# Turning layer 1's upper blocks by VectorE and DMAs instead of TensorE, with a new order of tokens

## The chip, the cores and the metric

The kernel runs on one core of a Trainium2 chip. The metric is the device time of one execution in microseconds (us); the median of three runs of the kernel before is 3070.16 us (3066.79 to 3072.19). TensorE multiplies matrices, VectorE and ScalarE work on elements and reductions, GpSimd does small arithmetic, and SyncE issues nearly all DMAs, in its program's order.

## The reference

The input x has 4 images of 128 channels and 64 x 64 = 4096 positions, in float32. Layer 0 is a convolutional attention with a gate; layer 1 is a self-attention over the positions as tokens, followed by a normalised recurrence over the tokens.

```
x = x + conv_attention(group_norm(x))              # q, k: 64 channels; v, gate: 128
t = tokens(x)                                      # [4, 4096, 128]
h = layer_norm(t); q = h @ W; scores = q @ q.T     # the scores are symmetric
t = t + softmax(scores) @ h
wx = batch_norm(layer_norm(t) @ Wf.T)
y[i] = sigmoid(wx[i] + y[i-1] @ V.T)               # over the 4096 tokens
x = from_tokens(t + y)
```

## The kernel before, in words

Each image goes through layer0 and layer1, four times in all; then one recurrence runs over all images. Work is tiled in blocks of 512 tokens (QB; NB = 8 per image), each of 4 tiles of 128 tokens (NQ).

Layer 0 (attention, lines 200 to 244, and layer0, 388 to 473) runs over 8 query blocks and 16 pairs of key tiles. Scores (L223) and weighted values (L403) use half the rows of TensorE each, two at a time. When a block ends, its finish appends small functions to the list `pending`: sums, denominators, projection, tokens. One of them is taken after a step of the main loop, which spreads the work; `ahead` holds the preparation of the next image, which takes the steps that `nothing` leaves.

A block is exchanged between channels-by-tokens and tokens-by-channels by `move` (L255 to L266): VectorE turns each 32 x 32 piece (L261), one DMA writes the result to a DRAM tile turn_d (L264), and four DMAs read it back, one for each group of 32 partitions (L266). Layer 0 uses it three times a block: for x, for the projected output, and for the normalised tokens into qt.

Layer 1 (layer1, L475 to L716) uses the symmetry of the scores. For query block n it computes score blocks (n, a) for a from n down to 0 (L672), takes the exponential on ScalarE with a row sum (L678), and multiplies with h (L539, `direct`). For a < n the same block is also needed turned, as (a, n): VectorE turns its pieces into dd (L683), sixteen DMAs on SyncE's queue exchange the 32-row groups into tt (L710), and four steps later TensorE multiplies it with h (L552, `reversed_products`) while VectorE sums it (L557). dd has two buffers and tt three. The order of n is 6, 7, 5, 4, 3, 2, 1, 0. `part` adds a product to oacc (L566) and `count` calls finish(n) when all parts of block n are there. In the last image the pair (1, 0) isn't turned but computed twice (`order`, `turns`).

finish(n) of layer 1 (L579 to L651) appends tokens, result, turn and inputs to `pending`. tokens turns oacc on TensorE (L608, four turns of 128 x 128 into PSUM), divides by the row sums and adds the old tokens (L610), and normalises into h2 (L276 to L280, GpSimd L131 and L132 for the root). result turns the new tokens back on TensorE (L621), copies them on ScalarE (L624) and stores them in t2_d (L625). turn does the same with h2 (L630, L631) into th, and inputs multiplies by the recurrence's weights (L635), takes the statistics (L636) and stores the product (L639 or L643).

A scheduler of the tile framework puts the instructions into each engine's order and sets the waits; an engine then runs its list strictly in order. `fast` and its tiles are set up in conv_attn_hybrid_kernel; the tail after all images is L763 to L850.

Of the kernel before, what the change touches and what calls it, by code (L numbers as in the profile page):

```python
# [10 lines left out]
F32 = mybir.dt.float32  # L11
I32 = mybir.dt.int32
AF = mybir.ActivationFunctionType
ALU = mybir.AluOpType
# [35 lines left out]
def conv_attn_hybrid_kernel(  # L50
# [14 lines left out]
    wxs_d = dram.tile([B, P, L // 2, G, 2], F32, name="wxs_d")  # L65
    t_d = dram.tile([B, NB, P, 4, NQ, 32], F32, name="t_d")

    turn_d = [dram.tile([P, 4, NQ, 32], F32, name=f"turn{i}_d") for i in range(8)]
    t2_d = dram.tile([B, C, N], F32, name="t2_d")
    wx_d = dram.tile([B, C, N], F32, name="wx_d")  # L70

# [86 lines left out]
def fast(  # L158
# [13 lines left out]
    with ExitStack() as st:  # L172
# [79 lines left out]
                nc.tensor.matmul(m[:, r, :cols], lhsT=lhsT[rs], rhs=rhs[rs], start=True, stop=True)  # L252
            return m[:, 0, :cols], m[:, 1, :cols]

        def move(blocks, dst):  # L255

            nonlocal n_moves
            d = work.tile([P, 4, NQ, 32], F32, tag="d", name="d", bufs=2)  # L260
            nc.vector.transpose(d.rearrange("q a j i -> q j a i"), blocks)  # L261
            via = turn_d[n_moves % len(turn_d)]
            n_moves += 1
            nc.sync.dma_start(via, d)  # L264
            for a in range(4):
                nc.sync.dma_start(dst[bass.ts(a, 32)], via[:, a].rearrange("(p i) j k -> i p j k", p=4))  # L266

        n_moves = 0

# [15 lines left out]
        def tiles(t):  # L285

            return [t[:, :, j, :] for j in range(NQ)]

        def quarters(t):
            return [t[:, j, :].rearrange("q (p i) -> q p i", p=4) for j in range(NQ)]  # L290
# [97 lines left out]
        def layer0(b, gate, q, k, v, need):  # L388
# [20 lines left out]
            def finish(n, o, acc):  # L409
                cs, ts = bass.ts(n, QB), bass.ts(n, NQ)  # L410
                og = work.tile([P, QB], F32, tag="og", name="og")
                nc.scalar.copy(og, o[1])
                nc.vector.tensor_tensor(og, o[0], og, ALU.add)
                nc.vector.tensor_tensor(og, og, gate[:, cs], ALU.mult)
                rinv = stat.tile([P, NQ], F32, tag="rinv", name="rinv")
                xb = work.tile([P, QB], F32, tag="xb", name="xb")
                t = work.tile([P, 4, NQ, 32], F32, tag="t", name="t", bufs=2)
                yt = work.tile([P, 4, NQ, 32], F32, tag="h2", name="yt")
                nc.sync.dma_start(xb, x[b, :, cs])
                nc.gpsimd.tensor_scalar(xb, xb, bpc, None, ALU.add)  # L420

                sub = stat.tile([P, NQ, 4], F32, tag="sub", name="sub", bufs=2)

                def sums():


                    half, blocks = acc[:, 0, :], acc[:, 1, :]
                    nc.vector.tensor_tensor(half, half, blocks, ALU.add)
                    nc.vector.transpose(blocks, half)
                    nc.vector.tensor_reduce(  # L430
                        sub, blocks.rearrange("q (j f k) -> q j f k", j=NQ, f=4), AX.X, ALU.add
                    )
                    move(xb.rearrange("c (j f k) -> c j f k", j=NQ, f=4), t)

                def denominators():
                    m0, m1 = halves(quart, sub.rearrange("q j f -> q (j f)"))
                    tot = stat.tile([P, NQ, 4], F32, tag="tot", name="tot", bufs=2)
                    flat = tot.rearrange("q j f -> q (j f)")
                    nc.vector.tensor_copy(flat, m0)
                    nc.vector.tensor_tensor(flat, flat, m1, ALU.add)  # L440
                    nc.vector.tensor_tensor(
                        tot, tot,
                        own.rearrange("q (j f) -> q j f", j=1).to_broadcast([P, NQ, 4]), ALU.mult,
                    )
                    den = den_all[:, b * NT + n * NQ : b * NT + (n + 1) * NQ]
                    nc.vector.tensor_reduce(den, tot, AX.X, ALU.add)
                    nc.vector.reciprocal(rinv, den)

                def projection():
                    m0, m1 = halves(wt["ps"], og)  # L450
                    nc.scalar.copy(og, m1)
                    nc.vector.tensor_tensor(og, m0, og, ALU.add)
                    move(og.rearrange("c (j f k) -> c j f k", j=NQ, f=4), yt)

                def tokens():
                    for j in range(NQ):
                        nc.vector.scalar_tensor_tensor(  # L457
                            t[:, :, j, :], yt[:, :, j, :], rinv[:, j : j + 1], t[:, :, j, :],
                            ALU.mult, ALU.add,
                        )  # L460
                    nc.sync.dma_start(t_d[b, n], t)
                    layernorm(tiles(t), quarters(h[:, ts, :]))

                    move(
                        h[:, ts, :].rearrange("q j (p i) -> q j p i", p=4),
                        qt[:, cs].rearrange("c (p j k) -> c p j k", j=NQ, p=4),
                    )
                    done.add((b, n))

                pending.extend([sums, nothing, denominators, projection, nothing, tokens])  # L470
# [4 lines left out]
        def layer1(b, h, qt):  # L475
# [52 lines left out]
            def order(n):  # L528


                return [0, 1] if b == B - 1 and n == 0 else list(range(n, -1, -1))

            def turns(n, a):
                return a < n and not (b == B - 1 and n == 1)
# [37 lines left out]
            def count(n):  # L572


                parts[n] += 1
                if parts[n] == NB - (b == B - 1 and n < 2):
                    finish(n)

            def finish(n):  # L579
                cs = bass.ts(n, QB)  # L580
                rinv = stat.tile([P, NQ], F32, tag="rinv", name="rinv")
                t = work.tile([P, 4, NQ, 32], F32, tag="t", name="t1", bufs=2)
                if b == B - 1 and n == 0:

                    one, two = (ep.tile([P, 2, QB], F32, tag="e", name="last") for _ in range(2))
                    h2, t1 = (one[:, r, :].rearrange("q (j c) -> q j c", j=NQ) for r in range(2))
                    th, t2 = two[:, 0, :], two[:, 1, :]

                    def bank():
                        return ps_s.tile([P, 2, QB], F32, tag="s", name="ml")[:, 0, :]  # L590
                else:
                    h2 = work.tile([P, NQ, C], F32, tag="h2", name="h2")
                    th = work.tile([P, QB], F32, tag="th", name="th")
                    t1 = work.tile([P, NQ, C], F32, tag="og", name="t1b")
                    t2 = None

                    def bank():
                        return ps_m.tile([P, QB], F32, tag="m", name="m1")
                nc.sync.dma_start(t, t_d[b, n])

                def tokens():
                    at = (B + b) * NT + n * NQ
                    den = den_all[:, at : at + NQ]
                    nc.vector.tensor_reduce(den, slots[:, bass.ts(n, NQ), :], AX.X, ALU.add)
                    nc.vector.reciprocal(rinv, den)
                    m = bank().rearrange("q (j c) -> q j c", j=NQ)
                    for j in range(NQ):
                        nc.tensor.transpose(m[:, j, :], oacc[:, n, bass.ts(j, P)], ident)  # L608
# [6 lines left out]
                    layernorm(quarters(t1), quarters(h2))  # L615

                def result():
                    nonlocal t2
                    m = bank()
                    for j in range(NQ):  # L620
                        nc.tensor.transpose(m[:, bass.ts(j, P)], t1[:, j, :], ident)  # L621
                    if t2 is None:
                        t2 = work.tile([P, QB], F32, tag="xb", name="t2")
                    nc.scalar.copy(t2, m)  # L624
                    nc.sync.dma_start(t2_d[b, :, cs], t2)  # L625

                def turn():
                    m = bank()
                    for j in range(NQ):
                        nc.tensor.transpose(m[:, bass.ts(j, P)], h2[:, j, :], ident)  # L630
                    nc.scalar.copy(th, m)  # L631

                def inputs():
                    m = bank()
                    nc.tensor.matmul(m, lhsT=wt["f"], rhs=th, start=True, stop=True)  # L635
                    nc.vector.bn_stats(bn_st[:, b * NB + n, :], m)  # L636
                    m = m.rearrange("p (g i s) -> p i g s", i=L // 2, s=2)
                    if b == B - 1:
                        nc.vector.tensor_copy(wxs[:, :, b, bass.ts(n, GB), :], m)  # L639
                    else:  # L640
                        wx = work.tile([P, L // 2, GB, 2], F32, tag="wx", name="wx")
                        nc.vector.tensor_copy(wx, m)
                        nc.sync.dma_start(wxs_d[b, :, :, bass.ts(n, GB), :], wx)  # L643

                if b == B - 1 and n == 0:
                    pending.appendleft(tokens)
                    pending.extend([result, turn, inputs])
                elif b == B - 1 and n < 4:
                    pending.extend([tokens, result, turn, inputs])
                else:  # L650
                    pending.extend([tokens, result, nothing, nothing, turn, inputs])  # L651


            for n in [NB - 2, NB - 1] + list(range(NB - 3, -1, -1)):
# [4 lines left out]
                for a in order(n):  # L659
# [4 lines left out]
                    for i in range(2):  # L664
# [31 lines left out]
                        clock += 1  # L696
                        if len(fifo) > LAG:
                            direct()
                            if a == n and i == 0:
                                direct()  # L700
                        if turned and turned[0][0] <= clock:
                            reversed_products()
                        if pending:
# [67 lines left out]
    with ExitStack() as st:  # L771
# [29 lines left out]
        def bank(k, s):  # L801
            return banks[s][k % 3][:, : HB * G].rearrange("p (b g) -> p b g", g=G)
# [450 lines left out]
```

## Time and profile before

| | |
|---|---|
| median of three runs | 3070.16 us |
| the profiled execution, and its span | 3067.95 us, 3066.1 us |
| TensorE busy, matmul instructions | 3000.1 us, 10834 |
| VectorE busy | 1882.3 us |
| ScalarE busy | 1154.7 us |
| L608, L621, L630: turns in PSUM bank m | 124 each, 19.9, 18.9 and 21.1 us, and 4 each in the last block |
| L624 and L631: copies on ScalarE | 32 each, 0.586 us each |
| L261: turn of 128 x 512 on VectorE | 96, 0.70 to 0.71 us each |
| DMAs tt<-dd (L710) | 1776 of 64 KB, 2.0 us to landing |
| DMAs turn_d<-d (L264), t, yt, qt<-turn_d (L266) | 96 of 256 KB, 384 of 64 KB, 2.0 to 2.1 us |
| DMAs t_d<-t and t_d<-last (L625) | 32 of 256 KB |

In the profile's lists a line gives the source line, the engine, the operation, what is written and read, and the count; PE is TensorE, PEld its loading of weights, DVE VectorE, ACT ScalarE, POOL GpSimd, SPq SyncE's queue. A name is given without its number, so that t2_d appears as t_d. A float32 matmul of the program is two instructions in the profile; a turn (L608, L621, L630) is one. The first number after the bar is busy time, then the mean of one in ns, then the engine's idle time ahead of it and what ended it.

### The profile page before, as it was taken

The numbers are of one execution on the slowest core, as the hardware profiler recorded it, in microseconds if no ns is written. First come the engines' busy times: TensorE is split into PE (matmuls) and PEld (weight loads), VectorE is DVE, ScalarE is ACT, GpSimd is POOL, SyncE is SP. The second block draws the span as 40 slices with busy tenths as digits, with TensorE's granted clock in tenths as the row PEclk, the third lists the DMA queues.
The fourth block names the chain that finished last, engine by engine and source line by source line (L and its number), as shares of the span: only waits on it lengthen the run. The fifth ranks groups of instructions, "written<-read, shape, count | busy, mean of one in ns | idle before, by whom it ended". The sixth has DMA issues, their size and how long they took to land.

```text
span 3066.1 us, 32642 instructions
## 1 busy us (share of the span) xinstructions
PE 3000.1 (98%) x10834; PEld 1377.5 (45%) x10834; DVE 1882.3 (61%) x3160; ACT 1154.7 (38%) x2148; POOL 148.3 (5%) x187
## 2 busy tenths in 40 slices
PE   7999999999999999999999999999999999999996
PEld 3444444444444444444444444444444444444443
DVE  6666665655666666655567666655566666455556
ACT  3444433333344443333344443333334444323334
POOL 0000000000000000000000000000000000000000
PEclk9999999999999999999999999999999999999998
DMA  1011143433211123333311113333321112543333
GB/s 52 28 56 56 42 115 86 99 93 92 53 56 55 41 82 96 93 96 92 85 46 61 39 50 112 88 96 93 94 61 52 46 49 90 139 104 93 99 111 159
DMA packets 233171, 241.17 MB, mean 79 GB/s; under 512 B 88480, under 2 KB 144288, under 8 KB 231968
## 3 DMA queue, kind: packets, MB, share of 16 engines
q1 hardware_dynamic: 231984, 238.18, 27.8%
q8 instruction: 89, 1.46, 0.2%
q14 instruction: 90, 0.74, 0.1%
q10 hardware_dynamic: 1008, 0.79, 0.1%
HBM read 65.80 MB, written 56.62 MB: 40 GB/s over the span
## 4 chain that ended last, share of the span: by engine, by line
PE 95%; DVE 3%; ACT 1%; POOL 0%; DMA 0%; issue 0%; ACTq 0%; SPq 0%; DVEq 0%; POOLq 0%
PE o L403 29%; PE o L539 16%; PE ps L223 15%; PE ps L672 14%; PE ot L552 12%; PE m L252 1%; PE m L635 1%; PE mq L497 1%; PE ps L505 1%; PE mp L335 1%; PE mp L370 1%; PE mp L355 1%; DVE ps_r L810 1%; DVE t2s L837 1%; PE m L630 1%; PE m L608 0%
## 5 line engine op out<-in xcount | busy, mean ns | idle before, releaser
L403 PE MATMUL o<-e,nxt 64*128 64x512 f32 x4096 | 964.8, 590 | 0.0
L225 ACT ACTIVATE e<-ps 128x1024 f32<-128x1024 f32 x512 | 521.6, 1025 | 678.2 <-PE ps L223 653.2
L232 DVE TENSOR_TENSOR acc<-acc,e 128x1024 f32<-128x1024 f32 x448 | 547.6, 1222 | 237.4 <-ACT e L225 221.6
L403 PEld LDWEIGHTS o<-e,nxt 64*128 64x128 f32 x4096 | 399.6, 187 | 483.4 <-issue 475.1
L678 ACT ACTIVATE e<-ps,shift 128x512 f32<-128x512 f32 x516 | 350.4, 683 | 670.0 <-PE ps L672 506.1
L539 PE MATMUL o<-e,h 128*128 128x512 f32 x1160 | 539.5, 592 | 0.0
L223 PE MATMUL ps<-nxt 64*128 64x512 f32 x2048 | 535.8, 597 | 2.2 <-ACT e L225 2.2
L672 PE MATMUL ps<-qt 128*128 128x512 f32 x1032 | 490.9, 595 | 2.9 <-ACT qt L498 2.7
L552 PE MATMUL ot<-tt,h 128*128 128x512 f32 x888 | 399.5, 592 | 0.0
L683 DVE STREAM_TRANSPOSE dd<-e 128x512 f32<-128x512 f32 x444 | 287.2, 687 | 87.9 <-ACT e L678 75.3
L539 PEld LDWEIGHTS o<-e,h 128*128 128x128 f32 x1160 | 218.3, 190 | 266.5 <-issue 261.9
L223 PEld LDWEIGHTS ps<-nxt 64*128 64x128 f32 x2048 | 194.4, 187 | 231.2 <-issue 158.9
L672 PEld LDWEIGHTS ps<-qt 128*128 128x128 f32 x1032 | 187.8, 190 | 213.0 <-issue 188.0
L552 PEld LDWEIGHTS ot<-tt,h 128*128 128x128 f32 x888 | 168.0, 190 | 209.5 <-issue 206.8
L557 DVE TENSOR_REDUCE slots<-tt 128x4 f32<-128x2048 f32 x111 | 250.8, 2260 | 9.8 <-DMA tt<-dd 9.2
L566 DVE TENSOR_TENSOR oacc<-oacc,ot 128x512 f32<-128x512 f32 x87 | 59.7, 686 | 187.0 <-PE ot L552 186.9
L131 POOL TENSOR_SCALAR rstd<-mv 128x4 f32<-128x4 f32 x64 | 14.5, 227 | 2429.7 <-DVE mv L277 2429.7
L678 ACT ACTIVATION_READ_ACCUMULATOR e<-ps,shift 128x1 f32 x516 | 101.3, 196 | 0.0
L457 DVE SCALAR_TENSOR_TENSOR t<-yt,rinv,t 128x128 f32<-128x128 f32 x128 | 36.6, 347 | 71.1 <-DMA yt<-turn_d 71.1
L420 POOL TENSOR_SCALAR xb<-xb,bpc 128x512 f32<-128x512 f32 x32 | 60.9, 1904 | 321.0 <-DMA xb<-in_x_dram 311.3
L132 POOL TENSOR_TENSOR rstd<-rstd,mhalf 128x4 f32<-128x4 f32 x64 | 66.4, 1037 | 5.3
L280 DVE TENSOR_SCALAR h<-t,mv,rstd 128x128 f32<-128x128 f32 x128 | 35.7, 344 | 47.0 <-POOL rstd L132 47.0
(160 smaller groups left out, 1659.5 us busy)
## 6 DMA issues: line engine op xcount, KB each, us to landing
tt<-dd SPq DMA_DIRECT2D x1776, 64.0 KB, 2.0
turn_d<-d SPq DMA_DIRECT2D x96, 256.0 KB, 2.0
t_d<-t SPq DMA_DIRECT2D x63, 256.0 KB, 2.0
nxt<-in_x_dram SPq DMA_DIRECT2D x16, 512.0 KB, 5.6
xb<-in_x_dram SPq DMA_DIRECT2D x32, 256.0 KB, 2.9
t<-turn_d SPq DMA_DIRECT2D x128, 64.0 KB, 2.0
yt<-turn_d SPq DMA_DIRECT2D x128, 64.0 KB, 2.0
qt<-turn_d SPq DMA_DIRECT2D x128, 64.0 KB, 2.1
```

Of the source, the lines that this page charges most:

```text
L132: nc.gpsimd.tensor_tensor(dst, dst, mhalf[:, :n], ALU.pow)
L223: nc.tensor.matmul(ps[:, h, :], lhsT=lhsT, rhs=rhs, start=True, stop=True)
L225: nc.scalar.activation(e, ps, AF.Exp, scale=scale)
L232: nc.vector.tensor_tensor(acc, acc, e, ALU.add)
L403: nc.tensor.matmul(o[r], lhsT=v[rs, p + h * PAIRS, :], rhs=e[rs, h, :], start=(p == 0 and h == 0), stop=(p == PAIRS - 1 and h == 1),)
L420: nc.gpsimd.tensor_scalar(xb, xb, bpc, None, ALU.add)
L539: nc.tensor.matmul(o, lhsT=h[:, NQ * a + 2 * i + half, :], rhs=e[:, half, :], start=(a == order(n)[0] and i == 0 and half == 0), stop=(a = ...
L552: nc.tensor.matmul(ot, lhsT=h[:, NQ * n + j, :], rhs=t[:, :, j, :, :].rearrange("q p k j -> q k p j"), start=(j == 0), stop=(j == NQ - 1),)
L557: nc.vector.tensor_reduce(slots[:, bass.ts(n, NQ), a], t.rearrange("q p b k j -> q b p (k j)"), AX.XY, ALU.add,)
L672: nc.tensor.matmul(ps[:, half, :], lhsT=qt[:, bass.ts(at, P)], rhs=qt[:, bass.ts(n, QB)], start=True, stop=True,)
L678: nc.scalar.activation(e[:, half, :], ps[:, half, :], AF.Exp, bias=shift, accum_out=slots[:, at, n : n + 1],)
L683: nc.vector.transpose(d.rearrange("q f b k j -> q k b f j")[:, 2 * i + half], e[:, half, :].rearrange("q (b f j) -> q b f j", b=NQ, f=NQ),)
```

## The change

`move` is written anew on a helper, turn_out. VectorE's turn stays; now four DMAs write, one for each group f of 32 partitions of d, into every row of the DRAM tile at a column offset, and one DMA reads the tile back as it lies. To fit, the order of tokens inside a block is changed in layer 0's views (f before j), in the sums of the denominators and where th is read. turn_out also writes straight to t2_d.

In layer 1, blocks n of 3 and above (4 and above in the last image) now finish through finish_moved: oacc is exchanged by a move (sums), the new tokens are made in place, h2 is exchanged by a move into th, and t goes to t2_d by a turn_out. Two empty places stand between sums and tokens and between tokens and inputs. The other blocks keep the turns of oacc and h2 on TensorE; their new tokens go to t2_d by a turn_out in place of the turn on TensorE, the copy and the store. reciprocals and recurrence_inputs are parts of the old code, now shared.

In the last image, block 0 takes a = 1 before a = 0, and a score block computed twice is counted for block a once its exponentials have been issued, so that finish(1) comes after it.

```diff
-            nc.sync.dma_start(via, d)
-            for a in range(4):
-                nc.sync.dma_start(dst[bass.ts(a, 32)], via[:, a].rearrange("(p i) j k -> i p j k", p=4))
+        def turn_out(blocks, dst):
+            d = work.tile([P, 4, NQ, 32], F32, tag="d", name="d", bufs=2)
+            nc.vector.transpose(d.rearrange("q a j i -> q j a i"), blocks)
+            for f in range(4):
+                nc.sync.dma_start(
+                    dst.rearrange("(a i) m -> i a m", a=4)[:, :, bass.ts(f, P)],
+                    d[bass.ts(f, 32)].rearrange("i a j k -> i a (j k)"),
+                )
+        def move(blocks, dst):
...
+            turn_out(blocks, via)
+            nc.sync.dma_start(dst, via)
...
-                    move(xb.rearrange("c (j f k) -> c j f k", j=NQ, f=4), t)
+                    move(xb.rearrange("c (f j k) -> c j f k", j=NQ, f=4), flat(t))
...
-                return [0, 1] if b == B - 1 and n == 0 else list(range(n, -1, -1))
+                return [1, 0] if b == B - 1 and n == 0 else list(range(n, -1, -1))
...
-                if parts[n] == NB - (b == B - 1 and n < 2):
+                if parts[n] == NB - (b == B - 1 and n == 0):
                     finish(n)
+            def finish_moved(n):
...
+                nc.sync.dma_start(t, t_d[b, n])
+                def sums():
+                    ot = work.tile([P, 4, NQ, 32], F32, tag="og", name="otk")
+                    move(oacc[:, n, :].rearrange("c (j f k) -> c j f k", j=NQ, f=4), flat(ot))
+                def tokens():
+                    reciprocals(n, rinv)
+                    for j in range(NQ):
+                        nc.vector.scalar_tensor_tensor(
+                            t[:, :, j, :], ot[:, :, j, :], rinv[:, j : j + 1], t[:, :, j, :],
+                            ALU.mult, ALU.add,
+                        )
+                    h2 = work.tile([P, 4, NQ, 32], F32, tag="h2", name="h2m")
+                    layernorm(tiles(t), tiles(h2))
+                    th = work.tile([P, QB], F32, tag="th", name="thm")
+                    move(h2.rearrange("q p j i -> q j p i"), th)
+                    turn_out(t.rearrange("q p j i -> q j p i"), t2_d[b, :, cs])
+                def inputs():
+                    recurrence_inputs(n, th, ps_m.tile([P, QB], F32, tag="m", name="mw"))
+                pending.extend([sums, nothing, nothing, tokens, nothing, nothing, inputs])
...
             def finish(n):
+                if n >= (4 if b == B - 1 else 3):
+                    return finish_moved(n)
...
                 def result():
-                    m = bank()
-                    for j in range(NQ):
-                        nc.tensor.transpose(m[:, bass.ts(j, P)], t1[:, j, :], ident)
-                    nc.scalar.copy(t2, m)
-                    nc.sync.dma_start(t2_d[b, :, cs], t2)
+                    turn_out(t1.rearrange("q j (p i) -> q j p i", p=4), t2_d[b, :, cs])
...
                     nc.scalar.copy(th, m)
+                    result()
...
-                    pending.extend([result, turn, inputs])
+                    pending.extend([turn, inputs])
                 elif b == B - 1 and n < 4:
-                    pending.extend([tokens, result, turn, inputs])
+                    pending.extend([tokens, turn, inputs])
                 else:
-                    pending.extend([tokens, result, nothing, nothing, turn, inputs])
+                    pending.extend([tokens, nothing, nothing, turn, inputs])
...
-                            if a == n and i == 0:
+                            if a == order(n)[0] and i == 0:
                                 direct()
+                        if a > n and i == 1:
+                            count(a)
```

## The prediction

> **What bounds the kernel now.** I read the page first, then the groups of TensorE by line and shape, then TensorE's instructions in order of time around one finished block, then SyncE's queue in order of time, because the change takes work from TensorE and gives it to VectorE and to that queue. From the page:
>
> ```profile
> PE 3000.1 (98%) x10834; PEld 1377.5 (45%) x10834; DVE 1882.3 (61%) x3160; ACT 1154.7 (38%) x2148; POOL 148.3 (5%) x187
> ...
> PE   7999999999999999999999999999999999999996
> ...
> DVE  6666665655666666655567666655566666455556
> ...
> PE 95%; DVE 3%; ACT 1%; POOL 0%; DMA 0%; issue 0%; ACTq 0%; SPq 0%; DVEq 0%; POOLq 0%
> ```
>
> TensorE is busy in every slice but the first and last, and 95% of the chain that ended last is its own. So a TensorE instruction taken out is worth its slot, if nothing new makes TensorE wait. The groups of TensorE by shape (busy us, mean ns of one, then idle before it):
>
> ```profile
> L672 PE MATMUL ps<-qt 128*128 128x512 f32 x1032 | 490.9, 595 | 2.9 <-ACT qt L498 2.7
> L630 PE MATMUL m<-ident,h 128*128 128x128 f32 x124 | 21.1, 283 | 2.2 <-DVE h L280 1.8
> L608 PE MATMUL m<-ident,oacc 128*128 128x128 f32 x124 | 19.9, 275 | 0.0
> L621 PE MATMUL m<-ident,t1b 128*128 128x128 f32 x124 | 18.9, 275 | 0.0
> ```
>
> The mean of one (275 ns) is no price, since matmuls overlap. The price is the distance between starts, here around one set of four turns:
>
> ```profile
> 512.56 1.02 PE L539 MATMUL o<-e,h 128*128 128x512 f32 x2
> 513.42 0.60 PE L608 MATMUL m<-ident,oacc 128*128 128x128 f32 x4
> 513.85 1.02 PE L539 MATMUL o<-e,h 128*128 128x512 f32 x2
> ```
>
> Four turns hold TensorE from 513.42 to 513.85, 0.43 us; two 512-wide instructions hold it 0.86 us. SyncE's queue in the last image's layer 1 (start, length, count):
>
> ```profile
> 2633.84 81.94 SPq L710 DMA_DIRECT2D tt<-dd  x125
> 2715.88 0.53 SPq L625 DMA_DIRECT2D t_d<-t  x1
> 2716.51 42.05 SPq L710 DMA_DIRECT2D tt<-dd  x64
> 2758.60 0.58 SPq L599 DMA_DIRECT2D t<-t_d  x1
> 2759.29 10.02 SPq L710 DMA_DIRECT2D tt<-dd  x16
> 2774.05 0.33 SPq L625 DMA_DIRECT2D t_d<-t  x1
> ```
>
> Sixteen issues for one pair of blocks take 10.0 us (0.633 us apart), and from 2633 to 2758 the queue hardly rests. This is the second resource, and the change loads it.
>
> **What the skill says.** The Trainium skill, "VectorE: DVE Perf Modes", section "The three transpose paths": VectorE turns independent 32x32 blocks only, while TensorE turns a whole 128x128 into PSUM. The trace agrees in form: L261 turns 128x512 in 0.71 us and DMAs finish the exchange between partition groups. "DMA: Bandwidth & Descriptors", section "Anatomy of one DMA": a DMA has about 2 us of fixed cost, mostly the wait for completion. The trace agrees: turn_d<-d, yt<-turn_d and tt<-dd all land 2.0 us after issue, and a write followed by its read costs about 4. Same page, "Issuing engines are not separate DMA queues": issuing time on the sequencer is "usually small relative to the DMA itself". Here it is not small: 1776 issues at 0.633 us are 1124 us of SyncE.
>
> **The change part by part.**
>
> *TensorE.* Moved blocks are 5 in each of three images and 4 in the last, 19 of 32; they lose the turns of L608 and L630, and all 32 blocks lose L621. That is 4 x (19 + 19 + 32) = 280 turns, 70 sets at 0.43 = **29.9 us off the path**, with no cover: TensorE has no holes there. In layer 0, half-height matmuls run in pairs, and starts in the trace show 0.31 us lost on entering and again on leaving a full-height one. The built order has 116 such changes instead of 122, so **-1.9 us**. Beside their slots, the sets of L630, L608 and L621 among full-height matmuls start or end late by some 7 us[...]; about 4 us of that belongs to removed sets: **-4 us**.
>
> *ScalarE.* 19 copies of L631 and 32 of L624 at 0.59 us go, 30 us. ScalarE is 38% busy; I count nothing, and if it were on the path this would only help.
>
> *VectorE.* Added: three turns per moved block (sums, h2, t) and one per other block, 19 x 3 + 13 = 70 at 0.70 = 49 us; multiply-adds and normalisation stay in number. It is 60% busy in layer 1 (79.85 of the 133 us from 487 to 620, by the table of windows), so 2.1 us per moved block lies beside TensorE's work. Nothing counted; if VectorE had no room it would be at most 49 us. The new multiply-add waits for its DMA (ot), and behind it stand the turns into dd and the additions that free the banks of ot. In the built order it stands 2.6 us of TensorE work after SyncE's read issue, which lands in about 2.6; about level.
>
> *SyncE.* A moved block adds two moves of five issues and one turn_out of four, and loses one store: 13 net. The nearest row is yt<-turn_d, 64 KB in pieces of 512 bytes too, from DRAM to 32 partitions: 0.43 us, 0.475 from start to start; 13 x 0.475 = **6.2 us**. Other blocks add 3, 1.4 us. A write of this shape by 32 partitions is not in the trace: bounds 0.33 (a single store) and 0.633 (as tt<-dd), so 4.3 to 8.2 us per block. Room: from 487.5 to 774.1 (22 pairs) SyncE needs 22 x 10.13 + about 9 = 232 of 287, 55 free; five moved blocks ask 31, and TensorE gets 8 shorter, leaving 16. In the last image, 2633.8 to 2940.2, it needs 413 x 0.633 + 5 = 266 of 306, 40 free; four moved blocks and a turn_out ask 26, TensorE gets 8 shorter, leaving 6. Pairs now land mostly 6 to 14 us before TensorE reads them (issued to 522.1, landed 523.6, read 532.9), but only 0.4 us before at 2675.0 in the last image. Adding my queue sums and TensorE's slots side by side in the built order, the last image's room falls by about 10 us over the three pairs around each h2 move and then recovers. I charge **+4 us** of TensorE waits there and none in the first three; bounds 0 and 20.
>
> The wait of the read on its four writes is covered in the built order by three tt<-dd issues (1.9 us) between; uncovered it would be 2 us of queue each. The wait of TensorE's L624 on th: 3.4 to 3.8 us of TensorE work follow the read issue, which needs 2.6; covered unless SyncE runs late. If it does, everything on TensorE stands behind it.
>
> *Layer 0's moves.* Same five issues, four writes and one read instead of one and four: 0.34 + 2.0 + 1.4 + 2.0 before, 1.4 + 2.0 + 0.35 + 2.0 after: **0**, bounds -2 and +2 per image.
>
> *The end.* Block 0 of the last image takes key block 1 first, and block 1 is finished only when those scores exist. In the built order block 1's turns now follow the last product; before they stood ahead of four of its instructions (2961.1). VectorE then has both blocks' multiply-add, statistics and normalisation (3.7 us) and a turn in one row. From the last product to the last inputs' matmul was 9.7 us (2965.0 to 2974.7); laid out with the same durations, counted from the last product: addition to 0.9, block 1's multiply-add to 2.0, statistics to 3.3, turn to 4.0, GpSimd's root to 5.3, normalisation with block 0's multiply-add between to 7.3, statistics and block 1's bn_stats (waiting for its matmul) to 9.3, root to 10.7, normalisation and turns to 12.2, copy to 12.8: **+3 us**, bounds 0 and +5. The last store, four issues and 2 us, lands before the bias of the recurrence is ready: 0.
>
> **Sum.** -29.9 - 1.9 - 4 + 4 + 3 = -28.8. The profiled execution took 3067.95 (span 3066.1): 3039.2. The median is 2.2 above it: **3041**.
>
> **Rivals.** *SyncE becomes the bound, slower.* If issues cost 0.633 and each of the two reads stalls the queue for 2 us, a moved block costs 8.2 + 4 = 12.2 us. Five ask 61 of 47 (55 less 8): 14 over, three times; the last image asks 49 + 2 of 32: 19 over. 61 us of TensorE waiting against a saving of 33 (35.8 less the end's 3): 3070 - 33 + 61 = **3098**. Waiting begins at about 9 us a moved block and passes the saving at 10.7 (19 x 10.7 - 171 = 33). For it: the 81.94 us run above. Against: yt<-turn_d at 0.43 and the fill between write and read. *Half is given back.* Slack is used up at each move in the last image and VectorE waits on ot or on dd, 15 us more: **3056**. For: the 0.4 us at 2675. *Nothing comes off*: the turns lay in TensorE's waits, or new ones of 29 us take their place: **3070**. Against: 0.43 us of undisturbed slot.
>
> **How the numbers follow.** Forecast 66%, 3031 to 3052 (SyncE bounds, end, waits); half back 14%; nothing 5%; SyncE bound 15%. The range 3031 to 3067 takes the first two. About 0.2%, 6 us, is what a measurement can tell from no change. Faster 0.80, same 0.05, slower 0.15.
>
> **What would show it.** Right: 52 turns each at the token and h2 lines, none for t; TensorE idle in layer 1 as small as now; th and ot waits under a few us; the new writes near 0.43 us. Wrong: TensorE or VectorE waiting on tt, th or ot by tens of us, writes over 0.6 us, or SyncE without a pause through layer 1; an end stretch longer by over 5 us.

## The result, and the profile after

The changed kernel takes 3141.87 us (median of 4, 3134.9 to 3148.68) against 3069.86 us: a ratio of 1.0235 (1.0211 to 1.026), 72 us slower. The forecast was 3041, with 3031 to 3067 as its range; even the rival that ended slower (3098) was too fast. The profiled execution is the fastest of the four and spans 3132.8 us, 66.7 more than before; the sums below are of this one. From its page, the lines that answer to those shown of the kernel before:

```profile
PE 3004.7 (96%) x10554; PEld 1360.2 (43%) x10554; DVE 1919.3 (61%) x3230; ACT 1125.9 (36%) x2097; POOL 150.1 (5%) x187
...
PE   7999999899999999999999999989999999999985
...
PE 88%; SPq 4%; DVE 3%; ACT 2%; DMA 1%; issue 1%; POOL 0%; DVEq 0%; ACTq 0%
```

The 280 turns are gone (10834 instructions have become 10554), and yet TensorE's share of the chain falls from 95% to 88%: SyncE's queue has 4%, ScalarE 2% instead of 1, and DMAs 1% instead of 0. Two slices inside layer 1 read 8 and no longer 9. TensorE's groups by shape say where it waited (the figures after the second bar are its idle time ahead of the group, and for what):

```profile
L710 PE MATMUL ps<-qt 128*128 128x512 f32 x1032 | 487.4, 597 | 7.8 <-ACT e L716 3.3 <-ACT qt L504 2.7
L558 PE MATMUL ot<-tt,h 128*128 128x512 f32 x888 | 405.4, 600 | 7.7 <-DMA tt<-dd 5.5 <-issue 2.2
L344 PE MATMUL mp<-nxt,w 128*128 128x512 f32 x60 | 34.9, 666 | 6.4 <-DVE nxt L369 2.4 <-DVE nxt L356 1.7 <-DVE wx L631 1.6
L364 PE MATMUL mp<-w,nxt 128*128 128x128 f32 x192 | 34.1, 331 | 20.1 <-DVE nxt L356 15.3 <-DVE nxt L369 4.7
L379 PE MATMUL mp<-nxt,w 128*128 128x512 f32 x48 | 26.4, 631 | 15.6 <-ACT nxt L380 15.6
L624 PE MATMUL mw<-thm,w 128*128 128x512 f32 x38 | 19.4, 592 | 0.0
L676 PE MATMUL m<-ident,h 128*128 128x128 f32 x48 | 10.5, 316 | 10.6 <-DVE h L286 10.6
```

L344, L364 and L379 are the next image's preparation (queries and keys, values, gate; L335, L355 and L370 before). The change doesn't touch them. Before, their lines were:

```profile
L335 PE MATMUL mp<-nxt,w 128*128 128x512 f32 x60 | 31.8, 611 | 2.5 <-DVE nxt L347 2.5
L355 PE MATMUL mp<-w,nxt 128*128 128x128 f32 x192 | 25.6, 276 | 0.0
L370 PE MATMUL mp<-nxt,w 128*128 128x512 f32 x48 | 25.5, 612 | 0.0
```

They waited 2.5 us in all before and wait 42.1 now, nearly always for the VectorE or ScalarE instruction that empties their PSUM bank (for bank m the program has a single buffer of 128 x 512 in PSUM, where TensorE writes its results). The moved blocks' own matmul (L624, mw<-thm) waits for nothing.

The idle column is not the whole loss. I took each distance from one TensorE start to the next and subtracted what that instruction takes in a stream (its slot: 0.427 us for 512 columns, 0.107 for 128, half of that with 64 rows). What is left over sums to 118.2 us before and 215.6 after: +97.4, against 29.9 of slots saved, which makes 67.5, the difference of the spans within 1 us. By place:

| lost time of TensorE, us | before | after |
|---|---|---|
| layer 1 of images 0, 1, 2 | 8.5 each | 33.4, 35.2, 33.0 |
| layer 0 of images 1, 2, 3 | 7.5 each | 10.7, 12.0, 12.0 |
| layer 1 of the last image, with the end | 16.8 | 25.2 |
| ahead of the preparation (L344, L364, L379), all images | 19.3 | 73.9 |

So 76 of the 97 us lie in layer 1 of the images that prepare another, and 55 stand ahead of the preparation itself. The last image, which prepares none, loses only 8 more than before. This is the stretch of TensorE in layer 1 of image 0:

```profile
555.78 0.59 PE L710 MATMUL ps<-qt 128*128 128x512 f32 x1
556.21 1.02 PE L624 MATMUL mw<-thm,w 128*128 128x512 f32 x2
557.07 1.02 PE L710 MATMUL ps<-qt 128*128 128x512 f32 x2
558.62 1.12 PE L344 MATMUL mp<-nxt,w 128*128 128x512 f32 x2 [0.52 <-DVE wx L631]
562.30 2.08 PE L364 MATMUL mp<-w,nxt 128*128 128x128 f32 x8 [2.56 <-DVE nxt L356]
565.16 2.08 PE L364 MATMUL mp<-w,nxt 128*128 128x128 f32 x8 [0.78 <-DVE nxt L369]
568.02 2.08 PE L344 MATMUL mp<-nxt,w 128*128 128x512 f32 x2 [0.78 <-DVE nxt L369]
569.88 4.46 PE L558 MATMUL ot<-tt,h 128*128 128x512 f32 x8
```

Four pieces of the preparation run one after another. All use the one bank m, so each waits until the one ahead of it has been read out. In the kernel before, 1.3 to 8.6 us of other matmuls lay between such pieces (the two of L355 follow at 555.25 and 557.44):

```profile
541.51 1.02 PE L335 MATMUL mp<-nxt,w 128*128 128x512 f32 x2
...
545.80 1.02 PE L335 MATMUL mp<-nxt,w 128*128 128x512 f32 x2
```

Just ahead of the bunch stands mw, a user of bank m as well. Its operand was asked for much earlier, as SyncE's queue shows:

```profile
517.53 18.23 SPq L750 DMA_DIRECT2D tt<-dd  x29
535.86 2.01 SPq L262 DMA_DIRECT2D turn_d<-d  x4
537.97 1.39 SPq L262 DMA_DIRECT2D t_d<-d  x3
539.53 0.34 SPq L272 DMA_DIRECT2D thm<-turn_d  x1
539.91 0.44 SPq L262 DMA_DIRECT2D t_d<-d  x1
540.45 10.01 SPq L750 DMA_DIRECT2D tt<-dd  x16
558.59 0.62 SPq L632 DMA_DIRECT2D wxs_d<-wx  x1
```

The read for th, issued at 539.53, landed at 542.4; mw starts 13.8 us after that. In the first three moved blocks of images 0 to 2 this lag is 12.9 to 15.0 us every time, in the last two 0.2 to 1.8, and in the last image 6 to 11. TensorE was not held up by data: in its list mw simply stands that late. And SyncE, at 550.5, has no more to do than to wait 8.1 us for the store wxs_d<-wx, which needs mw. The table of windows shows what the bunch costs (columns: us, TensorE busy, granted clock, DMA share, GB/s), first before and then after, in the same stretch:

```profile
556.00:590.00 34.00, 34.00 (x99) 1.00 0.35 91
```

```profile
556.00:590.00 34.00, 24.83 (x70) 0.85 0.37 86
```

TensorE loses 9.2 us of 34 to idling, and the clock is lower too. The Trainium skill, "TensorE: Matmul & The Clock Gate", Part 1, says that an idle TensorE falls back to half its clock until it has been busy again, and names an idle window of about 3.4 us for it. The trace agrees on the half: the granted clock is 0.50 from 561.4 to 571.6, and in layer 1 of images 0 to 2 some 67 full-height matmuls take twice their slot (11 us in all; 3 and 0.3 us before). It doesn't need so long a pause here: the longest hole of these stretches is 2.6 us, with short pieces of work between the holes.

My theory after this reading: in the order that was built, a moved block's mw has its turn for bank m as late as if its operand still travelled through SyncE's queue (on the chip it had landed); the preparation is behind it in the same bank, piles up, and then runs piece by piece with every emptying of the bank exposed. The rivals: the moves make VectorE or the DMAs slower for everybody; SyncE's queue is the bound (my forecast's own rival); layer 0's new moves or the last image's order cost the time.

### The profile page after: what moved, and what is told of

It reads as the page before. It is cut to its first block, busy times and chain, and to the rows that moved or that the text cites. A ratio compares the mean times of both kernels' runs of the same rounds, so it can differ in the third digit from the quotient of the medians.

```text
span 3132.8 us, 32678 instructions
## 1 busy us (share of the span) xinstructions
PE 3004.7 (96%) x10554; PEld 1360.2 (43%) x10554; DVE 1919.3 (61%) x3230; ACT 1125.9 (36%) x2097; POOL 150.1 (5%) x187
## 4 chain that ended last, share of the span: by engine, by line
PE 88%; SPq 4%; DVE 3%; ACT 2%; DMA 1%; issue 1%; POOL 0%; DVEq 0%; ACTq 0%
PE o L412 28%; PE o L545 14%; PE ps L223 14%; PE ps L710 12%; PE ot L558 11%; SPq L750 3%; PE m L252 1%; PE mp L364 1%; PE mp L344 1%; PE mq L503 1%; PE mp L379 1%; PE ps L511 1%; DMA tt<-dd 1%; DVE t2s L877 1%; DVE ps_r L850 1%
## 5 line engine op out<-in xcount | busy, mean ns | idle before, releaser
L545 PE MATMUL o<-e,h 128*128 128x512 f32 x1160 | 533.2, 592 | 0.0
L710 PE MATMUL ps<-qt 128*128 128x512 f32 x1032 | 487.4, 597 | 7.8 <-ACT e L716 3.3
L558 PE MATMUL ot<-tt,h 128*128 128x512 f32 x888 | 405.4, 600 | 7.7 <-DMA tt<-dd 5.5
L721 DVE STREAM_TRANSPOSE dd<-e 128x512 f32<-128x512 f32 x444 | 280.5, 681 | 31.5 <-ACT e L716 23.1
L710 PEld LDWEIGHTS ps<-qt 128*128 128x128 f32 x1032 | 189.5, 190 | 244.5 <-issue 200.0
L563 DVE TENSOR_REDUCE slots<-tt 128x4 f32<-128x2048 f32 x111 | 251.1, 2262 | 69.2 <-DMA tt<-dd 55.5
L558 PEld LDWEIGHTS ot<-tt,h 128*128 128x128 f32 x888 | 169.5, 193 | 220.3 <-issue 213.5
L523 ACT ACTIVATE e<-ps,shift 128x256 f32<-128x256 f32 x64 | 29.7, 469 | 110.8 <-PE ps L517 110.8
```

Of the source, the lines that this page charges most:

```text
L545: nc.tensor.matmul(o, lhsT=h[:, NQ * a + 2 * i + half, :], rhs=e[:, half, :], start=(a == order(n)[0] and i == 0 and half == 0), stop=(a = ...
L558: nc.tensor.matmul(ot, lhsT=h[:, NQ * n + j, :], rhs=t[:, :, j, :, :].rearrange("q p k j -> q k p j"), start=(j == 0), stop=(j == NQ - 1),)
L563: nc.vector.tensor_reduce(slots[:, bass.ts(n, NQ), a], t.rearrange("q p b k j -> q b p (k j)"), AX.XY, ALU.add,)
L710: nc.tensor.matmul(ps[:, half, :], lhsT=qt[:, bass.ts(at, P)], rhs=qt[:, bass.ts(n, QB)], start=True, stop=True,)
L721: nc.vector.transpose(d.rearrange("q f b k j -> q k b f j")[:, 2 * i + half], e[:, half, :].rearrange("q (b f j) -> q b f j", b=NQ, f=NQ),)
```

## Experiments: the bank, or the moves in themselves

Each kernel is the changed one with the edit shown, unless it says otherwise; each was timed with runs of the kernel before on the same chip, whose medians were 3067 to 3069 us.

**1. No block moved.**

```diff
-                if n >= (4 if b == B - 1 else 3):
+                if n >= NB:
```

> All of the change but the moved blocks: no block of layer 1 finishes by moves; all 32 keep their turns of oacc and h2 on TensorE, and t goes out by the turn_out; layer 0's new moves and the last image's new order stay. Theory (the moved block's last matmul waits for a DMA while it has its turn for the one PSUM bank m, and the next image's preparation piles up behind it and then runs back to back): the 54.6 us of longer gaps ahead of the preparation's matmuls are gone, and the time is that of before less 32 sets of turns (13.8 us), plus some 3 to 6 us at the end: 3055 to 3064. Rival (layer 0's new moves, two bytes of order in the tokens, or the last image's new order cost the time): the kernel stays above 3100.

Measured: 3079.51 us, ratio 1.0038 (1.0024 to 1.0052). The preparation waits 2.7 us instead of 42.1. So the moved blocks make the bunches. But the time is not the 3060 of the theory: with 13.7 us of turns fewer the kernel is 12 us slower than before. Something else in the change costs about 25 us here, and L676, the turn of h2, waits 8.7 us for VectorE's h against 2.2. Experiments 10 and 12 follow that.

**2. h2 turned on TensorE in the moved blocks**, sums and t still moved (finish_moved gets back the four turns and the copy into th, without the second move).

> In the moved blocks the sums are still exchanged by a move, and t still leaves by a turn_out, but h2 is turned on TensorE and copied by ScalarE as before, so that no matmul into bank m waits for a DMA. Theory (bank m): the gaps ahead of the preparation's matmuls fall from 77 to 25 to 45 us in sum; 51 sets of turns are saved (22 us), the SyncE queue has one move less a block: 3055 to 3085. Rival (moves of any kind delay VectorE, and the preparation's evacuations with it): the gaps stay at 70 us or more and the time above 3110.

Measured: 3080.26 us, 1.0039 (1.0025 to 1.0054). The waits of the preparation fall to 15.4 us (10.2 at the queries and keys, 5.2 at the gates), the time lost ahead of it from 73.9 to 33.7, as the theory had it. A move of the sums alone, whose reader is VectorE and not a matmul in bank m, leaves a third of these waits; what makes that third is not shown.

**3. The preparation in other banks.**

```diff
         def own_bank(_):
-            return ps_m.tile([P, 512], F32, tag="m", name="mp")
+            return ps_o.tile([P, 512], F32, tag="o", name="mp")
```

> The changed kernel with one word changed: the next image's preparation takes its PSUM banks from the pool of o (three banks, shared with the weighted values) and not from bank m. Theory (bank m): the preparation is no longer queued behind the moved block's last matmul; 30 to 50 us of its 55 us of added gaps go, and 3092 to 3112 is left, since the late matmul still holds up SyncE's store of its result. Rival (the preparation's gaps are the latency of VectorE and ScalarE in a busier layer 1): no bank helps, 3130 or more.

Measured: 3071.62 us, 1.0014 (1.0007 to 1.0021). This line takes 70 us off, more than I had given it. The moved blocks, their DMAs and VectorE's turns are all still there:

```profile
L558 PE MATMUL ot<-tt,h 128*128 128x512 f32 x888 | 400.4, 593 | 6.9 <-DMA tt<-dd 4.9 <-issue 1.9
...
L344 PE MATMUL mp<-nxt,w 128*128 128x512 f32 x60 | 31.3, 602 | 0.0
L364 PE MATMUL mp<-w,nxt 128*128 128x128 f32 x192 | 24.8, 275 | 0.0
L379 PE MATMUL mp<-nxt,w 128*128 128x512 f32 x48 | 24.0, 592 | 0.0
```

The preparation waits for nothing, the time lost ahead of it falls from 73.9 to 14.5 us, and layer 1 of images 0 to 2 loses 11.7, 10.0 and 9.6 us instead of 33 to 35. mw is as late as it was, or nearly: in the first three moved blocks of images 0 to 2 it starts 9.0 to 12.9 us after its operand has landed. So a late mw costs TensorE little where the preparation doesn't share its bank. "The moves slow everybody" falls here: VectorE's sums of tt even wait longer for it in this kernel (86.7 us, 55.5 in the changed one, 9.2 before).

**4. The same with the scores' banks** (tag "s" of ps_s in place of "o").

> As the run before, with the preparation's banks from the pool of the scores (two pairs of banks). Theory (bank m): the same gain, 30 to 50 us less than the changed kernel, if the scores do not wait much for a pair of banks that the preparation holds (38 pieces of some 2 us each): 3092 to 3115. Rival: 3130 or more.

Measured: 3098.12 us, 1.0101 (1.0084 to 1.0118). The preparation's waits are 0 here too, but the scores (L710) now wait 28.7 us for banks that it holds. Which bank is borrowed counts: the preparation gains the same, and over a third of it is paid back.

**5. mw in a bank of o, the preparation left in m.**

```diff
-                    recurrence_inputs(n, th, ps_m.tile([P, QB], F32, tag="m", name="mw"))
+                    recurrence_inputs(n, th, ps_o.tile([P, QB], F32, tag="o", name="mw"))
```

> The other half of the test: the changed kernel with the moved block's last matmul (mw) in a bank of o, and the preparation left in bank m. If mw's hold on bank m were all of it, the preparation would be free again: 3070 to 3095. Rival: with one bank for the preparation, anything that puts its pieces late in TensorE's order makes them run back to back there (mw in a bank of o now stands ahead of the weighted values in that pool's order); in the built order the first block's bunch is gone and two later ones remain, so 3095 to 3125.

Measured: 3110.84 us, 1.0148 (1.0132 to 1.0163): the rival's range. The pieces that used to pile up ahead of the first mw are apart again (L344 at 528.69 and 539.85, L364 at 544.14 and 553.62), but later ones still bunch, and the preparation waits 30.7 us. mw is as late as before (8.0 to 18.6 us in the first three moved blocks of images 0 to 2) and now has its place among the weighted products, in their pool. Taking mw out of bank m is worth 31 of the 72 us and no cure; what makes the later pieces bunch here is not shown.

**6. Control: the kernel before with the preparation in the banks of o.**

> Control: the kernel before with the preparation's banks from the pool of o, nothing else. If the bank only cures what the moved blocks do (theory), this is within 0.3% of the kernel before: 3062 to 3077. Rival (more banks make the preparation faster whatever the finish): about 25 us or more faster, 3045 or less.

Measured: 3069.94 us, 1.0005 (0.9996 to 1.0013). No difference. The bank is worth 70 us only where the moved blocks are; it repairs a harm and is no gain by itself.

## Experiments: SyncE's queue

**7. As 3, with the store of the inputs issued by GpSimd.**

```diff
-                    nc.sync.dma_start(wxs_d[b, :, :, bass.ts(n, GB), :], wx)
+                    nc.gpsimd.dma_start(wxs_d[b, :, :, bass.ts(n, GB), :], wx)
```

> The run with the preparation in the banks of o, and also the store of the recurrence's inputs (wxs_d<-wx) issued by GpSimd and not by SyncE. In the changed kernel SyncE stands up to 8.6 us at this store, because it waits for the moved block's late matmul, and tt<-dd issues stand behind it. Theory (that wait makes the last pairs of an image land late): 3 to 10 us less than with the store on SyncE, 3060 to 3069. Rival (SyncE makes it up, or the late pairs come from the added moves): within 3 us, 3069 to 3075.

Measured: 3062.01 us, 0.998 (0.9973 to 0.9987): 9.6 us less than 3. Layer 1 of images 0 to 2 now loses 7.5 us each, less than before the change, and the waits for tt (4.9) are 1.7. SyncE standing at the late store was a second cost of the late mw.

**9. The same store by GpSimd in the changed kernel**, bank m as it was.

> The changed kernel with the store wxs_d<-wx issued by GpSimd instead of SyncE, and the preparation left in bank m. Theory (two costs: bank m, about 60 us, and SyncE standing some 8 us at a block's store while tt<-dd issues wait behind it, about 10): the waits for tt ahead of the reversed products fall and 3120 to 3135 is left. Rival (SyncE's waits are the main cost and TensorE only follows): 3100 or less.

Measured: 3132.73 us, 1.0209 (1.0192 to 1.0226). The waits for tt go from 5.5 to 0.9; the preparation's stay (39.6). 9 us by the medians, though the intervals of the two ratios overlap. SyncE's waits are not the main cost.

**13 and 14. The moved blocks' DMAs issued by another engine**, all banks as in the changed kernel. turn_out and move take a queue, and the three calls in finish_moved pass it:

```diff
-                    move(oacc[:, n, :].rearrange("c (j f k) -> c j f k", j=NQ, f=4), flat(ot))
+                    move(oacc[:, n, :].rearrange("c (j f k) -> c j f k", j=NQ, f=4), flat(ot), nc.scalar)
...
-                    move(h2.rearrange("q p j i -> q j p i"), th)
-                    turn_out(t.rearrange("q p j i -> q j p i"), t2_d[b, :, cs])
+                    move(h2.rearrange("q p j i -> q j p i"), th, nc.scalar)
+                    turn_out(t.rearrange("q p j i -> q j p i"), t2_d[b, :, cs], nc.scalar)
```

> The changed kernel with the moved blocks' DMAs (four writes and a read for oacc, the same for h2, four writes for t) issued by GpSimd and not by SyncE; all banks as in the changed kernel. Theory (the moves are queued behind tt<-dd on SyncE, which puts the moved block's last matmul late in TensorE's order while it has bank m): in the built order the preparation's pieces are apart again, and the time falls to 3045 to 3075. Rival (any DMA ahead of a matmul in bank m does it): 3100 or more.

> As the run before, with ScalarE as the issuer of the moved blocks' DMAs. ScalarE is 36% busy, but its exponentials would stand behind an issue that waits for VectorE's turn or for the writes. Theory: the preparation is apart, and waits of ScalarE cost some: 3045 to 3090. Rival: 3100 or more.

Measured: GpSimd 3058.11 us, 0.9967 (0.9955 to 0.9979); ScalarE 3044.22 us, 0.9922 (0.9906 to 0.9937). With ScalarE the changed kernel, its banks untouched, is 97.7 us faster than with SyncE, 24.8 below before and 3 from my forecast (its theory had 3045 to 3090). Its TensorE around the same move:

```profile
538.53 1.02 PE L624 MATMUL mw<-thm,w 128*128 128x512 f32 x2
539.39 1.02 PE L545 MATMUL o<-e,h 128*128 128x512 f32 x2
540.25 1.02 PE L710 MATMUL ps<-qt 128*128 128x512 f32 x2
541.11 1.02 PE L344 MATMUL mp<-nxt,w 128*128 128x512 f32 x2
541.96 1.02 PE L710 MATMUL ps<-qt 128*128 128x512 f32 x2
...
547.97 1.05 PE L364 MATMUL mp<-w,nxt 128*128 128x128 f32 x8
```

mw starts at 538.53 and not at 556.21, 2.4 us after its operand landed (0.8 to 2.8 in image 0), and the preparation is spread as in the kernel before: it waits 5.0 us in all. Layer 1 of images 0 to 2 loses 9.4 us each. With GpSimd as issuer th lands 3.1 to 4.1 us after its issue in image 0, and TensorE waits 9.8 us for it (none with ScalarE).

The Trainium skill, "DMA: Bandwidth & Descriptors", section "Issuing engines are not separate DMA queues", says that issuing from several engines saves only the sequencer's time, "usually small relative to the DMA itself". The reads of image 0's moved blocks do land about as fast from SyncE (2.9 to 3.1 us) as from ScalarE (2.9 to 3.5). What changes is the place in a list that is full of tt<-dd, and here that decides 98 us. No run changed the place of mw alone.

## Experiments: the rest of the change

**8. The kernel before with the last image's new order alone** (order, the condition in count, and the count after the exponentials, as in the diff).

> The kernel before with the changed order of the last image alone (block 0 takes key block 1 first, block 1 finishes after those scores). The changed kernel's end shows 14.2 us from the last product to the last inputs' matmul, 9.7 before. Theory (the end alone): 3 to 6 us slower, 3071 to 3075. Rival (no effect without the turn_outs in the end): within 2 us.

Measured: 3069.59 us, 1.0002 (0.9994 to 1.001). No effect. From the last product to the last pass of the inputs' matmul: 11.1 us before, 11.3 here, 15.5 in the changed kernel.

**10. No block moved, and t turned on TensorE as before** (result gets back its four turns, ScalarE's copy, with its columns in the new order, and one store).

> No block of layer 1 moved, and t turned on TensorE and copied by ScalarE as before: what is left of the change is layer 0's new moves (four writes and one read), the new order of tokens and the last image's order. My prediction costs this at 0, bounds 2 us per image, and the end at 0 to 5: 3066 to 3075. Rival (layer 0's moves or the order cost what the run without moved blocks showed, 12 us and the 14 us of turns it saved): 3080 or more. If it is near before, those 26 us belong to the turn_out of t in place of TensorE's turn in blocks that are not moved.

Measured: 3067.84 us, 1.0 (0.9991 to 1.0008). Layer 0's new moves, the token order and the last image's order cost nothing together. What is left between this and run 1 (11.7 us, and 13.7 us of turns that run 1 saves) is turn_out in place of TensorE's turn of t: it costs 25 us for 32 blocks.

**11 and 12. As 7, with the first image's preparation back in bank m** (own_bank for prepare(0), a bank of o for prepare(b + 1)); **and then also result on TensorE in the 13 blocks that are not moved.**

> As the run with preparation in the banks of o and the store by GpSimd, but the first image's preparation stays in bank m (in banks of o it cost 5 us ahead of layer 1 in both kernels that had it). Theory: 4 to 6 us less, 3055 to 3059. Rival (run to run): no less, 3060 to 3064.

> As the run before it, and t of the 13 blocks that are not moved is turned on TensorE, copied by ScalarE and stored once, as in the kernel before. TensorE gets 13 sets of turns more (5.6 us). Theory (VectorE's turn into d lies inside the normalisation that TensorE's turn of h2 waits for, at the start of each layer 0 and at the end): 12 us of waits there and 4 us at the end go, 3044 to 3052. Rival (those waits come from the blocks finishing later): 3060 to 3065.

Measured: 3055.24 us, 0.9958 (0.9944 to 0.9971), and 3051.84 us, 0.9946 (0.9932 to 0.996). Eleven is 6.8 us below 7, a little more than its theory gave. Twelve has 5.5 us of turns more and is 3.4 us faster. L676's equivalent waits 3.6 us instead of 10.6, and the end is 12.1 us instead of 15.6. Of the theory's numbers (12 and 4) the first was too high; the places are right.

**15 and 16. Kernel 12 with the moves by GpSimd and by ScalarE.**

> The fastest kernel so far (preparation of the later images in the banks of o, the store of the inputs by GpSimd, t of the blocks that are not moved turned on TensorE; 3051.8) with the moved blocks' DMAs by GpSimd too. Of its waits the ones for tt in the last image (some 4 us) would go, if GpSimd's root of the variance does not come late behind its DMAs: 3044 to 3052. Rival (GpSimd's waits delay the roots, and h2 with them): 3056 or more.

> The same with ScalarE as the issuer: 3046 to 3056 if its exponentials are not held up; rival (they are, and the scores behind them): 3060 or more.

Measured: 3048.48 us, 0.9935 (0.9922 to 0.9949), and 3046.9 us, 0.9931 (0.9917 to 0.9944). Both within their theories' ranges, and 3 to 5 us below 12, though the intervals overlap.

**17 and 18. Kernel 14 with result on TensorE in the 13 blocks; and the store by GpSimd too.**

> The kernel with the moves issued by ScalarE, preparation in bank m and all stores on SyncE, and t of the 13 blocks that are not moved turned on TensorE as before (5.6 us of turns more). Theory (VectorE's turn of t lies in the way at the end): some 3 us at the end come off and nothing at the start of layer 0, where this kernel has no waits above those of before: 3043 to 3049. Rival (it is worth as much as with the moves on SyncE): 3036 to 3042.

> The same with the store of the inputs by GpSimd. With the last matmul 1 to 3 us after its operand, SyncE's store waits little, so that theory says no change, within 2 us of the run before it; the rival (the store still holds up tt<-dd) 3 us less or more.

Measured: 3049.42 us, 0.9937 (0.9923 to 0.9951), and 3045.03 us, 0.9925 (0.9911 to 0.9938). 17 lies just outside the theory: 5.5 us of turns come back and the end gives 2.0 (14.2 to 12.2). In kernel 14 the turn of t by VectorE is therefore the better choice, by the medians. The 4.4 us between 17 and 18 go against my expectation of none and fit the rival's 3 or more, but the runs of 18 reach from 3044 to 3049 and the profiled spans are 3046.8 and 3046.7: open. Kernel 14 is the fastest by its median and the simplest; 18 and 16 are not told apart from it.

## Why the prediction was wrong, point by point

- **The failed step** is the sentence on th: "3.4 to 3.8 us of TensorE work follow the read issue, which needs 2.6; covered unless SyncE runs late." It looked for a wait of TensorE at mw. There is none: L624 idles 0.0. In the last two moved blocks of images 0 to 2 the distance from the read's issue to mw is near the forecast, 3.2 to 4.9 us; in the first three it is 15.8 to 17.7, and mw was put 13 to 15 us behind its landed operand in TensorE's list. I also asked only who stands behind mw on TensorE, not who stands behind it for bank m. The sum has no term for the preparation, which I took to be unconcerned because its lines are not in the diff: it lost 54.6 us. Its new places could be read in the built order; I compared only the turns and the tt chain there.
- **The cause**, shown from both sides: giving the preparation another bank takes 70 us off though mw stays late (3, with 6 as control), and taking the moves off SyncE's queue takes 98 off though mw and the preparation share the bank, with mw early (14). Neither touches the number of turns, DMAs or bytes. That the scheduler puts mw so late because it expects th late behind the tt<-dd in SyncE's list is what the two orders suggest; I have not seen its costs, so that link is argued. The same holds for what makes later pieces bunch in 5.
- **TensorE -29.9: right.** 52 turns at L661, 52 at L676, none for t; the slots fall from 2910.7 to 2880.9 us. Changes between half and full height: 116 instead of 122, as the built order had it; losses of 0.31 us are seven or eight fewer, some -2.3 us (predicted -1.9).
- **The -4 for turns that start or end late: missed.** Where sets of turns lie among full-height matmuls, 8.0 us are lost at them in the changed kernel, as before (7.8), although 70 of 96 sets are gone: the sets that are left wait longer. In 14 it is 4.5, near the forecast.
- **SyncE's own costs: right.** The writes take 0.45 us in the median (predicted 0.43), the reads 0.34 to 0.45. The rival that SyncE becomes the bound named the right engine by the wrong mechanism: no queue without a pause (46 us of 287 are idle in layer 1 of image 0, 50 before), but one that made the order of another engine worse and then stood at a late store (about 9 us, runs 7 and 9).
- **Waits for tt in the last image, +4: about right.** L558 loses 2.0 us more there in the changed kernel, 4.4 in 14.
- **Layer 0's moves and the end.** 0 for layer 0 is right (10). The end is +4.4 (predicted +3, bounds 0 and 5), but not by the last image's new order that I blamed (8: +0.2): it comes with VectorE's turn of t (the end is 11.1 us in 10 and 15.6 in 1).
- **VectorE "nothing counted": wrong by 9 us or so.** It has room (61% busy), but its turn of t lies inside the normalisation that TensorE's turn of h2 waits for: L676 waits 10.6 us for h, 1.8 before. This is part of what layer 0's beginnings and the end lose. The turn of t is not enough by itself: 14 has the same turns, and there L676 waits 2.1 us. What else differs is open.
- **A sign that misled.** VectorE does wait on tt by tens of us, as the list of signs had it: 55.5 us in its sums, 9.2 before. That doesn't decide the time: in 14, the fastest kernel, it is 72.4.
- The forecast's arithmetic comes near where its premise holds: in 14, TensorE's lost time is 125.9 us, 7.7 above before, against 29.9 saved: 22 us less, where the sum had 28.8.

## What to carry to other kernels

When a step is turned from one engine's work into a DMA, ask not only who waits for the data but what the waiting instruction reserves: a PSUM bank with one buffer is a queue, and all its later users stand in it. In an order made by a scheduler, compare the places of all users of that bank, changed or not. And choose the issuer of a short move by what its list is full of: here a move that lands in 3 us, in a list of 1776 small DMAs, had its reader put 13 us late. The Trainium skill, "Perfetto Trace Analysis", section "Matmuls", advises independent groups of matmuls to rotate through different banks so that the emptying of one overlaps the next; this case puts 70 us on that in the kernel with moved blocks and nothing in the one before (6), and shows (4) that the banks have to come from a pool that has them to spare.

## What was not expected of the hardware

The reads of 256 KB from DRAM by `move` (L272) land in 2.5 to 4.5 us, median 2.8, against 2.0 for each of the four reads of 64 KB before. The four were issued one after another, and the last of them landed 3.3 to 3.5 us (median) after the first was issued, so one larger DMA saves issues and some 0.6 us. A whole move of layer 0, from the first write's issue to the last landing, still became longer, from 5.4 to 5.7 us in the median to 6.0 to 7.4; it cost nothing that 10 could show. Half clock after idling adds to the holes: 11 of the 97 us are matmuls that took twice their slot.
